# Quarter sums by token, a gate's product spread over the next block's steps, and a rebuilt start in a fused attention and FFN-gate kernel

## The chip, the cores and the metric

The kernel runs on one core of a Trainium2 chip. Its engines, as the profile names them: PE is TensorE (matmuls; PEld is its weight load), DVE is VectorE, ACT is ScalarE, POOL is GpSimd and SP is SyncE, which here only issues DMAs. Each engine runs its own instructions strictly in the order of the program and waits on semaphores for the others. The metric is device time in microseconds (us). Before the change it is 1982.35 us, the median of three runs (1981.34, 1982.35 and 1983.27).

## What is computed

x has 8 sequences of 256 tokens of width 512, 2048 tokens in all. It is normalized per token, goes through an attention with 128 heads and through a feed-forward gate, and the two are multiplied and added to x:

```
xn = (x - mean) / sqrt(var + 1e-5)
s  = attention(xn) @ Wo                    # q, k, v through latents of 64, and a rotary part of 64
lin(x, w, A, B) = x @ tile(w, (1, 4)).T + 0.5 * (x @ A.T @ B.T)       # A, B of rank 2
g  = silu(lin(silu(lin(xn, w1q, a1, b1)) * lin(xn, w3q, a3, b3), w2q, a2, b2))   # 512 -> 1376 -> 512
out = x + s * g
```

The weight matrix w1q has only 128 columns and is repeated four times, so `x @ tile(w1q).T` is (the sum of the four quarters of a token's row) times w1q. These quarter sums appear below. The low-rank part is two numbers per token and matrix, times b1 or b3.

## The kernel before

`first_phase` (L314 to L719) computes everything of the gate and the latents, in four blocks of 512 tokens, and takes about 219 us; the attention behind it, which the change leaves as it is, takes the rest of the 1982. There is no scheduler: the order in which the program emits instructions is the order on each engine. Tiles come from pools in which a name with one or two buffers is reused, so a new tile waits for the last user of the old one. PSUM has eight banks, handed out in turn by `bank`.

The start. `rows` (L357) receives the biases and the first row of each of the two weight matrices by three DMAs on ACT's queue. `warm(26)` (L617) runs 26 idle transposes on PE. Then four matmuls with only two rows, of two passes each (`spread_first`, L626), build "first" tiles that will be subtracted from the weights (`less_first`, `rest_less_first`), for this reason: the normed numbers of a token add up to zero, so a weight's first row can be subtracted from all its other rows. That frees row 0 of the weights and of xs0 and xs1 for the first of the two low-rank numbers (L505); the second is added by DVE (L541, L545). ACT copies the four results from PSUM. DVE gathers mean and variance of the four x tiles (L416, L417) and finds 1/sqrt by a bit shift and three Newton steps (L428 to L438), and norms the four tiles (L459).

Per block `tb` these functions follow each other:

- `load_x` loads four tiles of 128 tokens; `norm` and `norm_one` norm them in place. For blocks 1 to 3 the Newton steps are fourteen small operations on POOL (L440 to L450) and the norming is on ACT (L457).
- `turn` makes 16 PE transposes (L467) and copies them to `act1`, features by tokens.
- `sums` adds the four quarters: two additions on DVE (L479, L481), one on POOL (L480), one copy on ACT (L482), into xs0 and xs1.
- `narrow` (matmuls pm, L497 to L505) finds the low-rank numbers, sends them through DRAM and back as two tiles `low` broadcast to all partitions, and writes them into the first rows of xs0 and xs1.
- `down` (matmuls pp, L511) makes the latents, and `sum_x` has four subtractions on POOL (L158) and their DMAs.
- The loop over `u` = 0 to 5 calls `main(tb, u)`: two chunks (one in step 5) of 128 hidden units. PE makes px and py (L173, eight passes each), DVE adds the second low-rank number, times its column of b, to px (L541, "gate") and py (L545), ACT makes the silu of gate (L544), and POOL (L558) or DVE (L556, L551, L552) multiplies. px and py hold a PSUM bank until DVE has read it.
- `fold` adds four products into one on POOL (L570 to L572), `low_out` makes pm2 (L582).
- `gate_out` (L598) multiplies by w2 (matmuls pf, twelve passes a tile, four tiles), makes a silu on ACT into `gs`, which has two buffers (L608), and stores it (L609). It runs whole at the end of a block.

Among the steps of block `tb` stand the preparations for the next block: the norming of its tiles (steps 2 and 3 in block 0, steps 0 to 3 later), its turn (step 4), and, behind step 5, its `sums`, `narrow` and `down`. Block 3 has instead the first parts of the attention (`Project`, matmuls q) among its steps. `between(n)` puts loads and set-up of the attention at fixed places; `between(0)`, the largest on POOL, follows block 0.

## Time and profile before

| what | value |
|---|---|
| median of three runs | 1982.35 us |
| the profiled execution, its own time | 1983.69 us |
| its span, first to last instruction | 1981.9 us |
| mean granted TensorE clock in it | 0.998 |
| PE busy | 1964.4 us, 99% of the span |
| DVE, ACT, POOL busy | 1575.9, 1098.0, 758.3 us |
| the first matmul of the attention's scores starts at | 218.53 us |
| turn of block 0 starts (first xpt matmul) | 11.03 us |
| loop of block 0 starts (first px matmul) | 23.52 us |
| step 5 of blocks 0 and 1, px starts | 48.31 and 91.78 us |

A line of a group reads: source line, engine, operation, output and inputs by the program's names, count; then busy time, the mean of one in ns, and the idle time before it with what ended it. "PE py <- ACT gs" in the list of waits means that a matmul into py waited for the ACT instruction that works on gs. Matmul ends are modelled and neighbours overlap, so the time between starts is the better measure: eight passes of px or py take 0.86 us from start to start, a transpose 0.109 us at full clock and 0.213 at the start. PEclk is the share of full clock that was granted.

### The profile page before, as it was taken

Reading aid. Unit: us, or ns where it says so; the run is one execution under the profiler, and the core shown is the slowest. Engines: PE = TensorE matmul, PEld = TensorE weight load, DVE = VectorE, ACT = ScalarE, POOL = GpSimd, SP = SyncE. Lnnn points to the kernel's source line nnn. Section 1 sums busy time; section 2 is a strip of 40 time slices with the busy share of each in tenths; the row PEclk is TensorE's granted clock in tenths of the full one; section 3 lists DMA queues with packets and bytes.
Section 4 is the critical chain, followed back from the end, with each engine's and each line's share of the span. In section 5 each row is a group of like instructions: output and inputs, shape, how many; then the busy total and the mean of one; then the engine's idle time right before and its main releaser. Section 6 shows DMA issues by size and latency. Waiting matters only on the chain.

```text
span 1981.9 us, 78697 instructions
## 1 busy us (share of the span) xinstructions
PE 1964.4 (99%) x34033; PEld 1309.7 (66%) x34033; DVE 1575.9 (80%) x2666; ACT 1098.0 (55%) x3029; POOL 758.3 (38%) x1113
## 2 busy tenths in 40 slices
PE   8999999999999999999999999999999999999998
PEld 4334567767777766667776766667776767676775
DVE  7764678888787877788787878788787878888888
ACT  3333465566556555566556555566556555655654
POOL 5877445544552323332332323322332323233232
PEclk9999999999999999999999999999999999999999
DMA  6235322222232223322232322321232222122212
GB/s 195 100 118 179 114 87 87 77 77 87 75 125 89 100 87 101 100 85 68 87 103 89 99 87 101 100 84 69 87 104 88 99 87 86 67 87 87 72 50 87
DMA packets 120017, 187.02 MB, mean 94 GB/s; under 512 B 10715, under 2 KB 84843, under 8 KB 119673
## 3 DMA queue, kind: packets, MB, share of 16 engines
q1 hardware_dynamic: 119665, 181.97, 27.3%
q8 instruction: 270, 4.42, 0.9%
q14 instruction: 74, 0.61, 0.1%
q10 hardware_dynamic: 8, 0.02, 0.0%
HBM read 147.86 MB, written 34.10 MB: 92 GB/s over the span
## 4 chain that ended last, share of the span: by engine, by line
PE 93%; POOL 2%; DVE 2%; issue 1%; DMA 1%; ACT 0%; SPq 0%; POOLq 0%; ACTq 0%; DVEq 0%
PE q L173 40%; PE sc L828 35%; PE av L879 11%; PE po L173 2%; PE pf L173 1%; PE py L173 1%; PE qq L249 1%; PE px L173 1%; POOL h4b L571 0%; POOL hT L558 0%; DVE ring L854 0%; POOL h L570 0%; PE pm L173 0%; DMA xt<-in_x_dram 0%; PE pp L173 0%
## 5 line engine op out<-in xcount | busy, mean ns | idle before, releaser
L847 ACT ACTIVATE pr<-sc,nmx 128x256 f32<-128x256 f32 x2048 | 814.6, 500 | 463.3 <-DVE nmx L841 459.1
L841 DVE TENSOR_REDUCE nmx<-sc 128x2 f32<-128x512 f32 x1024 | 635.5, 683 | 281.7 <-PE sc L828 257.4
L854 DVE STREAM_TRANSPOSE ring<-pr 128x512 f32<-128x512 f32 x1024 | 635.0, 678 | 0.0
L216 POOL TENSOR_TENSOR e<-e,e 128x256 f32<-128x256 f32 x128 | 93.8, 733 | 1042.5 <-ACT e L211 558.8
L173 PE MATMUL q<-x,ws 128*32 128x256 f32 x8192 | 489.0, 379 | 0.7 <-POOL ws L137 0.7
L828 PE MATMUL sc<-act,qr 32*128 32x256 f32 x8192 | 488.3, 374 | 0.0
L828 PEld LDWEIGHTS sc<-act,qr 32*128 32x128 f32 x8192 | 420.7, 185 | 21.8
L173 PEld LDWEIGHTS q<-x,ws 128*32 128x32 f32 x8192 | 266.6, 110 | 176.3 <-POOL ws L137 1.1
L173 PE MATMUL q<-x,w 128*32 128x256 f32 x6144 | 381.7, 381 | 0.9 <-DVE py L545 0.8
L173 PEld LDWEIGHTS q<-x,w 128*32 128x32 f32 x6144 | 187.4, 110 | 155.6 <-ACT pr L847 35.6
L828 PE MATMUL sc<-kc,qcm 32*128 32x256 f32 x4096 | 280.7, 387 | 0.0
L828 PEld LDWEIGHTS sc<-kc,qcm 32*128 32x128 f32 x4096 | 198.0, 184 | 65.0 <-issue 50.4
L879 PE MATMUL av<-ring,vpad 128*32 128x256 f32 (+1 forms) x4160 | 233.4, 376 | 0.1
L211 ACT COPY e<-q 128x256 f32<-128x256 f32 x512 | 202.4, 396 | 26.5 <-PE q L173 26.5
L900 ACT ACTIVATE acc<-av,sides_sb 128x128 f32<-128x128 f32 (+1 forms) x172 | 60.5, 420 | 244.6 <-PE av L879 244.6
L879 PEld LDWEIGHTS av<-ring,vpad 128*32 128x32 f32 x4160 | 134.6, 110 | 88.3 <-issue 1.6
L269 POOL TENSOR_TENSOR qcm<-qc,mask_sb 128x1024 f32<-128x1024 f32 x64 | 122.2, 1910 | 0.0
L217 POOL TENSOR_TENSOR e<-e,e 128x256 f32<-128x256 f32 x128 | 93.6, 731 | 10.0
L218 POOL TENSOR_TENSOR qr<-e,e 128x256 f32<-128x256 f32 x128 | 93.5, 731 | 10.0
L310 POOL COPY vpad<-vall 32x128 f32<-32x128 f32 x256 | 75.4, 294 | 10.2 <-PE av L879 2.3
L228 DVE TENSOR_TENSOR qr<-e,q 128x256 f32<-128x256 f32 x128 | 53.9, 421 | 23.0 <-POOL e L216 17.5
L541 DVE SCALAR_TENSOR_TENSOR gate<-low,bcol_sb,px 128x512 f32<-128x512 f32 x44 | 32.8, 745 | 45.0 <-POOL hT L558 25.7
(124 smaller groups left out, 1138.0 us busy)
## 6 DMA issues: line engine op xcount, KB each, us to landing
w<-in_w_rope_dram SPq DMA_DIRECT2D x128, 512.0 KB
ws<-sums_d SPq DMA_DIRECT2D x96, 512.0 KB
sums_d<-ws SPq DMA_DIRECT2D x32, 512.0 KB
x<-xs_d SPq DMA_DIRECT2D x28, 256.0 KB
xt<-in_x_dram SPq DMA_DIRECT2D x16, 256.0 KB
xs_d<-xt SPq DMA_DIRECT2D x16, 256.0 KB
gate_d<-gs SPq DMA_DIRECT2D x16, 256.0 KB
g<-gate_d SPq DMA_DIRECT2D x16, 256.0 KB
```

Source lines behind the costliest of these rows:

```text
L173: nc.tensor.matmul(to[tile_], w[:, tile_], x, start=start, stop=stop, skip_group_check=True)
L211: nc.scalar.copy(self.e[i], self.banks[i])
L216: nc.gpsimd.tensor_add(m6, m6, m1)
L217: nc.gpsimd.tensor_add(m7, m7, m6)
L218: nc.gpsimd.tensor_add(self.out(1, 1), self.split(m7), self.split(m5))
L269: nc.gpsimd.tensor_mul(qcm, qks[b, sg // 2][0].rearrange("p (q i) -> p q i", i=32).unsqueeze(2).to_broadcast([P, 8, 4, 32]), mask_sb[:, ds ...
L310: nc.gpsimd.tensor_copy(vpad[rows, :, :, 8 * t + 4 * (sg % 2) :][..., :4], valls[b][rows, :, sg])
L828: nc.tensor.matmul(sc[r][:, h, :], lhs.rearrange("p t i -> p (t i)"), rhs, start=(part == 0 and h == 0), stop=(part == 2), skip_group_chec ...
L841: nc.vector.tensor_reduce(nmx[:, r, :], scs[n, f][r], AX.X, ALU.max, negate=True)
L847: nc.scalar.activation(p[:, h, :], scs[n, f][r][:, h, :], AF.Exp, bias=nmxs[n, f][:, r, h : h + 1])
L854: nc.vector.transpose(rings[r][:, (2 * n + f // 2) % 3].rearrange("p k q i -> p q k i")[:, ds(2 * (f % 2), 2)], prs.pop((n, f, r)).rearran ...
L879: nc.tensor.matmul(av[32 * r : 32 * r + 32, cols], vpad[:, k, r, :], rings[r][:, of, k].rearrange("p h q i -> p h (q i)"), start=(k == 0), ...
```

## The change

Four things are edited, all in `first_phase`.

1. The first rows. The biases and first rows of w1 lie in a tile `rows_0`, loaded on ACT's queue, those of w3 in a part of `w2_sb`, loaded on POOL's queue; w2 and b2 are therefore loaded later. 26 idle transposes become 2, and 2 behind the four first-row matmuls become 10. The matmuls go matrix by matrix. The first norm uses ACT's square root, DVE's reciprocal and one Newton step; it stands behind the first three of ACT's copies, and the fourth copy behind it.
2. Block 1's statistics, norming and loads are spread over earlier places. For blocks 2 and 3 `norm` moves from the end of the block before last to step 0.
3. The quarter sums of blocks 1 to 3: `add_quarters` reduces each normed tile from 128x512 to 128x128 on DVE, one step after its norming; behind the turn, in step 4, PE transposes the four results into one bank (`xst`) and ACT copies it twice. The three additions and the copy fall away; block 0 keeps them.
4. `gate_out` of blocks 0 to 2 is done one tile at a time at the head of steps 0 to 3 of the next block; that of block 3 stays whole at the end.

```diff
--- before.py
+++ after.py
@@
         f2 = pool("f2", 2, st)
         xts, xns, xnT, xsum, lows = {}, {}, {}, {}, {}
-        def load_x(tb):
-            xts[tb] = []
-            for n in range(4):
+        def load_x(tb, tiles=range(4)):
+            for n in tiles:
                 t = f1.tile([P, D], F32, tag="xt", name=f"xt_{tb}_{n}", bufs=6)
                 nc.sync.dma_start(out=t, in_=x[ds(tb * TB + n * P, P), :])
-                xts[tb].append(t)
+                xts.setdefault(tb, []).append(t)
@@
 
-        rows = f1.tile([P, 3 * TB], F32, tag="h4", name="rows")[:, 0:F]
-        nc.scalar.dma_start(out=rows[64:97:32], in_=b13[0:33:32, :])
-        for k, wt in enumerate((w1t, w3t)):
-            nc.scalar.dma_start(out=rows[65 + 32 * k : 66 + 32 * k], in_=wt[0:1, :])
+        rows = [
+            f1.tile([P, 3 * TB], F32, tag="h4", name="rows_0")[64:66, 0:F],
+            w2_sb.rearrange("p a m -> p (a m)")[96:98, 0:F],
+        ]
+        for k, (engine, wt) in enumerate(((nc.scalar, w1t), (nc.gpsimd, w3t))):
+            engine.dma_start(out=rows[k][0:1], in_=b13[32 * k : 32 * k + 1, :])
+            engine.dma_start(out=rows[k][1:2], in_=wt[0:1, :])
+
+        one = f2.tile([P, 1], F32, tag="sq", name="one")
+        nc.gpsimd.memset(one, 1.0)
+        nc.scalar.activation(one, one, AF.Sqrt)
         chunk_rows = f2.tile([P, TB], F32, tag="gs", name="chunk_rows")[:, 0:P]
         nc.gpsimd.memset(chunk_rows[0:32], 0.0)
@@
         nc.sync.dma_start(out=wdn_sb, in_=w_down.rearrange("(c p) m -> p c m", p=P))
         for w_sb, wt in ((w1_sb, w1t), (w3_sb, w3t)):
             load_chunks(nc.sync, w_sb, wt)
+        load_x(1, range(2))
...
@@
...
-        load_x(1)
+        load_x(1, range(2, 4))
         mvs = {}
@@
         def norm(tb):
 
-            for n in range(4):
-                norm_part(tb, n)
+            if tb != 1:
+                for n in range(4):
+                    norm_part(tb, n)
             mv = mvs[tb]
             ve = f2.tile([P, 4], F32, tag="ve", name=f"ve_{tb}")
             nc.vector.tensor_scalar_add(ve, mv[:, :, 1], EPS)
-            i0 = f2.tile([P, 4], I32, tag="i0", name=f"i0_{tb}")
-            nc.vector.tensor_single_scalar(i0, ve.bitcast(I32), 1, ALU.logical_shift_right)
-            r0 = f2.tile([P, 4], I32, tag="r0", name=f"r0_{tb}")
-            nc.vector.tensor_scalar(r0, i0, -1.0, float(0x5F3759DF), ALU.mult, ALU.add)
-            r = r0.bitcast(F32)
             e = f2.tile([P, 4], F32, tag="e", name=f"e_{tb}")
-            for step in range(3):
+            if tb:
+                i0 = f2.tile([P, 4], I32, tag="i0", name=f"i0_{tb}")
+                nc.vector.tensor_single_scalar(i0, ve.bitcast(I32), 1, ALU.logical_shift_right)
+                r0 = f2.tile([P, 4], I32, tag="r0", name=f"r0_{tb}")
+                nc.vector.tensor_scalar(r0, i0, -1.0, float(0x5F3759DF), ALU.mult, ALU.add)
+                r = r0.bitcast(F32)
+            else:
+                sq = f2.tile([P, 4], F32, tag="i0", name="sq")
+                nc.scalar.activation(sq, ve, AF.Sqrt)
+                r = f2.tile([P, 4], F32, tag="r0", name="r_first")
+                nc.vector.reciprocal(r, sq)
+            for step in range(3 if tb else 1):
                 new = f2.tile([P, 4], F32, tag=f"r{step}", name=f"r_{tb}_{step}")
                 if tb == 0:
                     nc.vector.scalar_tensor_tensor(e, r, -0.5, r, ALU.mult, ALU.mult)
@@
                 nc.scalar.activation(xn, xn, AF.Identity, bias=off[:, n : n + 1], scale=one)
...
+
+        quarters = {}
+
+        def add_quarters(tb, n):
+            if n == 0:
+                quarters[tb] = f1.tile([P, 4, P], F32, tag="quarters", name=f"quarters_{tb}")
+            nc.vector.tensor_reduce(
+                quarters[tb][:, n], xns[tb][n].rearrange("p (c s) -> p s c", c=4), AX.X, ALU.add
+            )
         def turn(tb):
             a = f1.tile([P, KT, TB], F32, tag="act1", name=f"act1_{tb}")
@@
             a = xnT[tb]
             xs = [f1.tile([P, TB], F32, tag=f"xs{k}", name=f"xs{k}_{tb}") for k in range(2)]
+            xsum[tb] = xs
+            if tb:
+                pt = bank(f"xst_{tb}")
+                for n in range(4):
+                    nc.tensor.transpose(pt[:, ds(n * P, P)], quarters[tb][:, n], ident)
+                for k in range(2):
+                    nc.scalar.copy(xs[k], pt)
+                return
             xs2 = f1.tile([P, TB], F32, tag="tmp", name=f"xs2_{tb}")
             nc.vector.tensor_add(xs[0], a[:, 0, :], a[:, 1, :])
+            norm_part(1, 0)
             nc.gpsimd.tensor_add(xs2, a[:, 2, :], a[:, 3, :])
             nc.vector.tensor_add(xs[0], xs[0], xs2)
             nc.scalar.copy(xs[1], xs[0])
-            xsum[tb] = xs
         def over_xn(tb, name, weights):
             ps = bank(f"{name}_{tb}")
@@
                 t = f1.tile([P, TB], F32, tag=f"low{k}", name=f"low{k}_{tb}")
                 nc.sync.dma_start(out=t, in_=low_d[tb][k : k + 1, :].to_broadcast([P, TB]))
                 lows[tb].append(t)
+            for k in range(2):
                 nc.scalar.copy(xsum[tb][k][0:1], mid[32 * k : 32 * k + 1])
             for j in range(4):
                 nc.sync.dma_start(
@@
                         to, m2[32 * q : 32 * q + 32], 0.5, to, ALU.mult, ALU.add
                     )
-        def gate_out(tb):
-            pfs = [bank(f"pf_{tb}_{n}") for n in range(4)]
+        def gate_out(tb, tiles):
+            pfs = {n: bank(f"pf_{tb}_{n}") for n in tiles}
             for ks in ((0, 1), (2,)):
-                for n in range(4):
+                for n in tiles:
                     for k in ks:
                         on_columns(
                             pfs[n], h4s[tb][:, k, ds(n * P, P)], w2_sb[:, k, :], k == 0, k == 2
                         )
-            for n in range(4):
+            for n in tiles:
                 gs = f2.tile([P, D], F32, tag="gs", name=f"gs_{tb}_{n}")
                 nc.scalar.activation(gs, pfs[n], AF.Silu)
                 nc.sync.dma_start(out=gates_d[4 * tb + n], in_=gs)
@@
             for n in range(count):
                 nc.tensor.transpose(idle[:, ds(n % 4 * P, P)], ident, ident)
-        warm(26)
+        warm(2)
...
-            parts.append(list(by_chunks(to, rows[64 + 32 * k : 66 + 32 * k])))
+            parts.append(list(by_chunks(to, rows[k])))
         def spread_first(k, ps, one, two):
             nc.tensor.matmul(
@@
             )
             return one, ps
-        for i in range(2):
-            for k in range(2):
+        copies = []
+        for k in range(2):
+            for i in range(2):
                 ps = bank(f"first_{k}_{i}").rearrange("p (q m) -> p q m", q=2)
-                nc.scalar.copy(*spread_first(k, ps, *parts[k][i]))
-        warm(2)
+                copies.append(spread_first(k, ps, *parts[k][i]))
+        warm(10)
+        for copy in copies[:3]:
+            nc.scalar.copy(*copy)
+        stats = norm(0)
+        nc.scalar.copy(*copies[3])
         def less_first(k, engine):
             w_sb = (w1_sb, w3_sb)[k]
@@
                 one = w_sb[:, 8:11][:, a, b]
                 nc.gpsimd.tensor_sub(one, one, firsts[k][:, 8:11][:, a, b])
-        stats = norm(0)
         for n in range(4):
             norm_one(0, n, *stats)
         turn(0)
         sums(0)
+        norm_part(1, 1)
         less_first(0, nc.gpsimd)
         narrow(0)
         less_first(1, nc.vector)
+        norm_part(1, 2)
+        norm_part(1, 3)
         between(-1)
-        for to, of in ((a2_sb, a2), (w2_sb, w2t), (w2_sb[96:98, 2, :], b2[0:2, :])):
-            nc.sync.dma_start(out=to, in_=of)
+        nc.sync.dma_start(out=a2_sb, in_=a2)
         down(0)
         ps = bank("bcol")[:, 0:32]
         nc.tensor.transpose(ps, chunk_rows[0:32], ident[0:32, 0:32])
         nc.scalar.copy(bcol_sb.rearrange("p c k -> p (c k)"), ps)
         rest_less_first(0)
         rest_less_first(1)
+        for to, of in ((w2_sb, w2t), (w2_sb[96:98, 2, :], b2[0:2, :])):
+            nc.sync.dma_start(out=to, in_=of)
+        stats = norm(1)
         for tb in range(NTB):
             more = tb + 1 < NTB
             for u in range(6):
+                if tb and u < 4:
+                    gate_out(tb - 1, [u])
                 pj = None
                 if not more and u >= 2:
                     pj = Project(u - 2)
@@
                 if u in (3, 5):
                     fold(tb, u // 2 - 1)
                     low_out(tb, u // 2 - 1)
-                if u == 1 and tb == 0:
-                    stats = norm(1)
                 if more:
                     for n in range(4):
-                        if u == (n if tb else 2 + n // 2):
+                        if u == (min(n + 1, 3) if tb else n) + 1:
+                            add_quarters(tb + 1, n)
+                    if u == 0 and tb:
+                        stats = norm(tb + 1)
+                    for n in range(4):
+                        if u == (min(n + 1, 3) if tb else n):
                             norm_one(tb + 1, n, *stats)
                 if u == 4 and more:
                     turn(tb + 1)
+                    sums(tb + 1)
                 if u == 1 and tb + 2 < NTB:
                     load_x(tb + 2)
                 if tb == NTB - 2 and u == 1:
@@
                 if not more:
                     between(u + 2)
             if more:
-                sums(tb + 1)
                 narrow(tb + 1)
                 low_out(tb, 2)
                 down(tb + 1)
             else:
                 low_out(tb, 2)
-            gate_out(tb)
+                gate_out(tb, range(4))
             if tb == 0:
                 between(0)
-            if tb + 2 < NTB:
-                stats = norm(tb + 2)
         nc.scalar.activation(cks_sb, cks_sb, AF.Exp)
         between(8)
```

## The prediction

> **What bounds the kernel now.** I read the page's busy table and chain first, then the busy time by stretch, then TensorE's (PE's) waits, then the order in time at the places that these name.

> The page, busy time and chain:

> ```profile
> span 1981.9 us, 78697 instructions
> PE 1964.4 (99%) x34033; PEld 1309.7 (66%) x34033; DVE 1575.9 (80%) x2666; ACT 1098.0 (55%) x3029; POOL 758.3 (38%) x1113
> PE 93%; POOL 2%; DVE 2%; issue 1%; DMA 1%; ACT 0%; SPq 0%; POOLq 0%; ACTq 0%; DVEq 0%
> ```

> PE is the bound, so a gain can only come out of its holes, and a new hole costs in full. By stretch (PE busy, then the other engines, PEclk, DMA share, GB/s):

> ```profile
> 0.00:11.00 11.00, 9.16 (x36) 5.89 (x36) 5.86 (x22) 3.53 (x5) 4.29 (x31) 0.89 0.88 236
> 11.00:24.00 13.00, 12.97 (x133) 7.79 (x137) 8.57 (x12) 4.63 (x12) 8.17 (x7) 0.83 0.46 143
> 24.00:59.00 35.00, 31.01 (x313) 10.80 (x309) 26.90 (x45) 13.29 (x23) 25.66 (x39) 1.00 0.46 149
> 59.00:102.00 43.00, 41.43 (x408) 14.62 (x404) 30.10 (x48) 17.00 (x28) 36.05 (x70) 1.00 0.34 114
> 102.00:146.00 44.00, 42.34 (x424) 14.99 (x420) 29.89 (x48) 17.00 (x28) 30.27 (x37) 1.00 0.40 133
> 146.00:219.00 73.00, 70.35 (x1008) 29.73 (x1004) 31.00 (x46) 23.93 (x50) 52.95 (x61) 1.00 0.42 144
> 219.00:1982.00 1763.00, 1757.17 (x31742) 1225.87 (x31736) 1443.59 (x2447) 1018.57 (x2886) 600.94 (x873) 1.00 0.27 89
> ```

> The rows are the start, the head of block 0, blocks 0 to 3, and the attention, which the edits leave alone. Up to 219 us PE idles 13.7 us, of which the head has 1.9 and block 0 has 4.0. PE's waits there (us, times, longest):

> ```profile
> PE py L173 <- ACT gs L608: 2.3, 2, 1.4
> PE py L173 <- DVE gate L541: 1.7, 1, 1.7
> PE px L173 <- DVE gate L541: 1.6, 3, 0.6
> PE q L173 <- DVE py L545: 0.8, 1, 0.8
> PE pf L173 <- DVE h L594: 0.5, 2, 0.3
> PE xpt L467 <- DVE xt L459: 0.4, 1, 0.4
> ```

> Waits on gs are the two-buffer store of the gate; waits on L541 and L545 are chunks whose PSUM banks DVE has not freed. The head in order of time (start, duration):

> ```profile
> 1.35 4.86 PE L615 MATMUL idle<-ident 128*128 128x128 f32 x26 [1.35 <-POOL ident masks.py:199]
> 6.13 3.87 PE L627 MATMUL first<-rows,others 2*128 2x512 f32 x8
> 11.03 3.68 PE L467 MATMUL xpt<-ident,xt 128*128 128x128 f32 x16 [0.41 <-DVE xt L459]
> ```

> and the group of first-row passes from 8.5 to 14.5 us (busy, mean ns):

> ```profile
> L627 PE MATMUL first<-rows,others 2*128 2x512 f32 x2 | 1.7, 954 | 0.0
> ```

> Idle transposes start 0.213 us apart up to 5.0 us, 0.109 after; the late first-row passes take 954 ns where earlier ones stood 0.43 apart. PEclk is 0.50 from 8.6 to 15.2, although PE was busy for 3.19 of the 3.30 us before 8.4, mostly with these two-row passes.

> **The change, part by part.** Durations are of this execution. It took 1983.69, 1.34 above the median 1982.35; I add the sum to the median.

> *Head.* The rows of the first tile land at 4.74 (biases at 3.87), instead of 7.23 for the last row. 26 idle transposes become 2, so the eight passes can start at about 4.8, but on a PE at half rate: 0.43 doubled is 0.86, and 0.954 was seen, so 6.9 to 7.6 us, to 11.7 to 12.4. The ten transposes behind them are 10 x 0.213 = 2.1, and the turn of block 0 starts at 13.8 to 14.5 instead of 11.03. The square root stands on ACT behind three copies, the third of which waits for six passes: 4.8 + 5.2 + 0.6 = 10.6. With root, reciprocal and one step (five small operations of 0.2) the rows are normed from 11.6 against 10.43, before PE asks for them: the nine Newton operations removed (8.66 to 10.39, 1.7 us) buy nothing. After 15.3 the clock was full in this trace; I take the same, since ten transposes and the turn fill the time ahead of it. Seven of 16 transposes then run at 0.213 and the rest at 0.109, so pm starts at about 16.4 instead of 14.64, while 0.33 that pm lost at half rate comes back. With the later passes +1.5 to +2.3: **+1.9**. Bounds: -1.0 if the passes run at 0.43 (they end at 8.3, rows normed from 9.3, turn at about 10, still at 0.213), +5 if the clock comes one step of 3.4 us later (the full times 5.1, 8.5, 15.3 are 3.4 apart or twice that). The POOL queue's two row loads have no row in this trace; ACT's issues took 0.21 to 1.10 and landed 2.9 to 3.1 later. These passes come third and fourth, after 8.2, so a load from POOL has 5 us beyond ACT's first landing to hide in; nothing, up to +1 if it takes twice ACT's time.

> [...]

> *Block 0.* Statistics of block 1 (four of 0.83) leave step 1 for places before the loop; DVE begins the loop 1.2 later (25.95 for 24.73). Newton for block 1 runs on POOL after the last subtraction: that queue is without a gap to 30.23, then 14 x 0.28 = 3.9, to 34.1. ACT's norm of tile 0 (0.75) waits for it, ahead of step 1's silu (0.63): step 1's product starts at 35.55. From there DVE has 12 gates and ups (0.66 apart), 7 products (0.68) and 4 quarter sums before the turned sums: 7.9 + 4.8 + 4 x 0.68 = 15.4, to 50.95. The quarter sum has no row here; the nearest is DVE's reduction of 128x512 (L841, 683 ns), which I take; bounds 0.35 and 1.35 (POOL's and DVE's large subtractions took 1.3). In the new order px of step 5 stands behind four transposes of these sums: 51.3 instead of 48.32. 0.5 of later holes (0.31 at 48.8, and part of its wait) closes: **+2.5**; down to 0 if the sums take 0.35 and POOL is earlier, +5 at 1.35.

> *Blocks 1 and 2.* Gone: waits for gs (0.74 and 1.1), pf's wait for the fold (0.4 and 0.46), because gate_out runs a tile at a time (1.29 us) at the head of steps 0 to 3. Its sixteen DMAs and silus are spread over the same queues; SP waits 23 us for gs now with nothing due behind. New: in step 4, PE has 1.74 of turn and 0.44 of sums' transposes, then waits. DVE after the last py: 0.66 + four products 2.7 + two sums 1.36, and 0.44 and latencies: 5.3. It comes to that late by 0.5 at least: step 3's product and sum (1.4) stand before step 4's first gate, whose matmul comes 0.86 later. So px of step 5 starts 5.8 after the last py, against 3.0 and 2.4 before. Hole, less what is gone and less the px and py holes of before (0.76, 0.66, 0.3): **+1.4 and +1.6**. Bounds -1.5 each (sums ready when the turn ends) and +3 each (DVE 3 us behind, as at 89.66, where it begins a gate whose matmul ended at about 86.4). POOL's and ACT's removed sums were beside other work: nothing.

> *Block 3.* No turn, no sums, and gate_out(2) is spread: 1.57 (gs), 1.05 (q behind py) and 0.44 (pf) go; gate_out(3) at the end stays with its 0.37: **-3.1**; bounds -3.1 and -1.

> Sum: +1.9 + 2.5 + 1.4 + 1.6 - 3.1 = +4.3, so 1982.35 + 4.3 = 1986.6.

> **Rivals.** (a) *The clock falls in the new holes.* Each leaves PE without work for some 3.6 us; the longest now is 1.87. A stretch of 3.4 us at half rate costs 1.7; in two of three blocks 3.4: 1990.0. For it: it fell at 8.5 with PE busy on small work. Against: 1.87 never did it. [...]

> (b) *First rows at full rate.* PEclk reads 1.00 from 0 to 8.5, so the 0.213 of the first transposes may be another thing than the clock. Head -1.0 instead of +1.9: 1983.7.

> (c) *Faster: the sums are not late.* 1.29 us more of PE work in each of steps 0 to 3 lets DVE run ahead (its gates waited 25.7 us for POOL's products), and sums land as the turn ends. Blocks 1 and 2 give -1.5 each, block 0 -0.5, with the head at +1.9 and block 3 at -3.1: -4.7, 1977.7. Each us by which the sums are earlier is worth 3 us; it decides when px of step 5 starts less than 2.5 after the last py. Against: the DVE work behind the last py adds up to 4.7 with no lateness at all.

> **How the numbers follow.** Forecast 0.47 (1984.5 to 1988.7), (a) 0.20, (b) 0.18, (c) 0.15. A measurement of this kernel tells about 0.2%, 3.96 us, from no change: same is 1978.4 to 1986.3. The forecast gives 0.28 slower and 0.19 same, (a) slower, (b) same, (c) 0.13 faster: faster 0.13, same 0.39, slower 0.48. Range from (c), a little cut, to (a): 1978.5 to 1990.5.

> **What would show it.** Right: eight first-row passes 0.86 to 0.95 apart from 4.8; the turn at 13.8 or later; PE waiting for DVE's quarter sum at the new transposes in blocks 0 to 2, some 3 to 3.6 us each; no wait for gs in blocks 1 to 3. Wrong: passes at 0.43, turn before 11; that wait below 1 us; PEclk below 1.00 after 24 us; a late row load from POOL that holds the third pair of passes.

## The result, and the profile after

The changed kernel takes 1996.55 us, median of six runs (1994.41 to 1998.07), against 1982.14 for the kernel before (six runs, 1981.34 to 1983.27). The ratio is 1.0073, with a 95% interval of 1.0063 to 1.0083: it is slower by 14.4 us, where 4.3 were forecast, and the time lies above the range. The side was right and the size was not.

The profiled execution of the changed kernel took 1995.62, 0.9 under its median. Its busy times on the page, and the busy time by stretch (PE, PEld, DVE, ACT, POOL, then PEclk, DMA share, GB/s):

```profile
span 1993.8 us, 78696 instructions
PE 1971.9 (99%) x34029; PEld 1318.6 (66%) x34029; DVE 1581.7 (79%) x2665; ACT 1100.6 (55%) x3034; POOL 754.5 (38%) x1113
```

```profile
0.00:11.00 11.00, 7.88 (x16) 3.77 (x17) 5.34 (x16) 3.93 (x7) 5.61 (x34) 1.00 0.92 252
11.00:24.00 13.00, 13.00 (x143) 8.44 (x145) 10.41 (x18) 5.35 (x14) 8.68 (x8) 1.00 0.51 136
24.00:59.00 35.00, 28.07 (x240) 9.33 (x236) 28.42 (x42) 13.40 (x22) 22.02 (x36) 0.85 0.45 146
59.00:102.00 43.00, 39.85 (x368) 12.91 (x364) 30.09 (x47) 16.36 (x27) 34.17 (x68) 0.95 0.35 114
102.00:146.00 44.00, 41.32 (x403) 14.07 (x395) 30.30 (x49) 17.06 (x29) 26.57 (x34) 0.97 0.40 133
146.00:219.00 73.00, 72.23 (x1026) 37.71 (x1029) 31.15 (x47) 23.59 (x48) 44.27 (x51) 0.96 0.39 130
```

PE is as busy as before, 99%, and that hides the loss: a PE at half clock is busy too. What tells is the column behind the engines, PEclk. It was 1.00 in the last four rows before and is 0.85, 0.95, 0.97 and 0.96 now. (The rows are cut where the blocks of the kernel before end. Up to the attention the granted clock was 0.50 three times, from 46.7 to 56.9, from 97.9 to 104.7 and from 145.7 to 152.5 us; the third time belongs to block 2.) And the largest of the waits behind the start, with one at the start (us, times, longest):

```profile
PE xst L505 <- DVE quarters L480: 9.8, 5, 3.5
PE first L659 <- POOL others L375: 1.8, 1, 1.8
PE xpt L490 <- DVE gate L573: 1.0, 1, 1.0
```

The waits for gs, for q behind py and for the fold are gone, as forecast; in their place stands one new wait, for the quarter sums, three times. Block 1 in order of time (start, duration), PE first and then DVE in the same stretch:

```profile
92.32 1.03 PE L173 MATMUL py<-xs,w_sb 128*32 128x512 f32 x8
93.28 1.97 PE L490 MATMUL xpt<-ident,xt 128*128 128x128 f32 x16
95.08 0.38 PE L505 MATMUL xst<-ident,quarters 128*128 128x128 f32 x2
98.14 0.47 PE L505 MATMUL xst<-ident,quarters 128*128 128x128 f32 x1 [2.68 <-DVE quarters L480]
99.09 0.47 PE L505 MATMUL xst<-ident,quarters 128*128 128x128 f32 x1 [0.47 <-DVE quarters L480]
99.49 1.94 PE L173 MATMUL px<-xs,w_sb 128*32 128x512 f32 x8
101.20 1.93 PE L173 MATMUL py<-xs,w_sb 128*32 128x512 f32 x8
102.91 1.94 PE L614 MATMUL pm<-hT,a_sb 128*32 128x512 f32 x8
```

```profile
96.36 0.69 DVE L584 TENSOR_TENSOR hT<-gate,py 32x512 f32<-32x512 f32 x1
97.07 1.96 DVE L480 TENSOR_REDUCE quarters<-xt 128x128 f32<-128x512 f32 x2
```

DVE comes to the last two quarter sums at 97.07, behind step 4's four products, and PE, whose turn ended at about 95.1, waits until 98.14 and 99.09. Then px and py of step 5 take 1.71 us from start to start instead of 0.86. That is half clock, and it holds until 104.7:

```profile
99.50:104.70 5.20, 5.20 (x29) 1.26 (x32) 1.83 (x3) 1.70 (x3) 0.00 (x0) 0.50 0.00 0
104.70:110.00 5.30, 5.30 (x88) 2.55 (x84) 1.80 (x3) 0.77 (x2) 3.99 (x4) 1.00 0.01 3
```

Block 2 repeats this, with the same waits of 2.68 and 0.47. In block 0 the wait is 3.53, from 48.2 to 51.74, but there the clock was already down when it began, at 46.7, behind two shorter waits of the turn:

```profile
44.47 0.63 PE L490 MATMUL xpt<-ident,xt 128*128 128x128 f32 x4 [0.78 <-DVE hT L588]
46.08 0.63 PE L490 MATMUL xpt<-ident,xt 128*128 128x128 f32 x4 [0.98 <-DVE gate L573]
51.74 0.48 PE L505 MATMUL xst<-ident,quarters 128*128 128x128 f32 x1 [3.53 <-DVE quarters L480]
```

The balance by stretch, from the starts of PE's instructions in the two profiled executions (a block runs from the end of its own pp, for block 0 from its first px, to the end of the next block's pp; block 3 to the first scores):

| stretch | before | after | difference | forecast |
|---|---|---|---|---|
| start, to the first px | 23.5 | 22.8 | -0.7 | +1.9 |
| block 0 | 35.5 | 42.1 | +6.6 | +2.5 |
| block 1 | 43.5 | 47.6 | +4.1 | +1.4 |
| block 2 | 43.0 | 47.7 | +4.6 | +1.6 |
| block 3 | 73.0 | 71.0 | -2.0 | -3.1 |
| attention | 1763.4 | 1762.7 | -0.7 | 0 |

The sum is 11.9. The profiled execution of before was 1.6 above its median and that of the changed kernel 0.9 below; that makes up the 14.4.

### The profile page after: what moved, and what is told of

The parts are those of the page before. It is cut to its first block, busy times and chain, and to the rows that moved or that the text cites. A ratio compares the mean times of both kernels' runs of the same rounds, so it can differ in the third digit from the quotient of the medians.

```text
span 1993.8 us, 78696 instructions
## 1 busy us (share of the span) xinstructions
PE 1971.9 (99%) x34029; PEld 1318.6 (66%) x34029; DVE 1581.7 (79%) x2665; ACT 1100.6 (55%) x3034; POOL 754.5 (38%) x1113
## 4 chain that ended last, share of the span: by engine, by line
PE 95%; DVE 2%; POOL 1%; issue 1%; DMA 0%; ACT 0%; POOLq 0%; DVEq 0%; ACTq 0%
PE q L173 39%; PE sc L872 34%; PE av L923 11%; PE po L173 2%; PE pf L173 2%; PE px L173 1%; PE py L173 1%; PE qq L249 1%; PE pm L173 1%; PE pp L173 1%; PE pm L614 0%; DVE ring L898 0%; PE vps L294 0%; DVE py L577 0%; PE first L659 0%
## 5 line engine op out<-in xcount | busy, mean ns | idle before, releaser
L173 PE MATMUL q<-x,ws 128*32 128x256 f32 x8192 | 491.0, 379 | 0.4 <-issue 0.3
L173 PEld LDWEIGHTS q<-x,ws 128*32 128x32 f32 x8192 | 269.2, 110 | 174.7 <-issue 0.8
L173 PE MATMUL q<-x,w 128*32 128x256 f32 x6144 | 383.0, 381 | 0.0
L173 PEld LDWEIGHTS q<-x,w 128*32 128x32 f32 x6144 | 190.2, 110 | 152.5 <-ACT pr L891 35.8
```

What stands on the lines that cost most here:

```text
L173: nc.tensor.matmul(to[tile_], w[:, tile_], x, start=start, stop=stop, skip_group_check=True)
```

## The experiments

The theory after the result, A: PE runs out of work at the xst transposes in three blocks, and the clock falls to half in each of these holes. Its rivals: B, the loss sits in the start or is spread over the engines, and the holes only show it; and the prediction's own view, that holes cost their length and nothing more. All times are medians beside runs of the kernel before on the same chip.

### The hole filled with idle work

```diff
                 pt = bank(f"xst_{tb}")
+                for n in range(30):
+                    nc.tensor.transpose(pt[:, ds(n % 4 * P, P)], ident, ident)
                 for n in range(4):
```

> The changed kernel, with 30 idle transposes (3.3 us at full clock) ahead of the four xst transposes in each of three blocks: the wait stays as long, but PE is busy in it. Theory A: the clock does not fall, so about 2.6 us come back in each block, 7.8 in all: 1988.7, between 1987 and 1991, and px and py of step 5 take 0.86 instead of 1.71. If the half rate comes from something else than the idle time (the work that follows, or the transposes themselves, which in the start of the kernel did lift the clock), nothing comes back: 1996.5, or more by what the 30 transposes add.

1988.91, ratio to before 1.0033 (1.0020 to 1.0045). Against the changed kernel 7.6 us come back, although PE reaches step 5 no earlier (7.1 us after the start of the last py in blocks 1 and 2 beside 7.2, and 11.0 beside 10.6 in block 0). The stretches around the same place in block 1:

```profile
93.00:98.00 5.00, 4.71 (x42) 4.36 (x40) 4.61 (x6) 1.95 (x5) 4.75 (x5) 1.00 0.63 210
98.00:103.00 5.00, 5.00 (x71) 2.25 (x74) 2.88 (x4) 1.70 (x3) 0.34 (x1) 1.00 0.02 3
```

PEclk is 1.00 through the filled hole and behind it in blocks 1 and 2. In block 0 the clock falls at the turn here too, at 47.3, but it is back at 50.7, within the idle transposes, where in the changed kernel it stayed down until 56.9 (PEclk over 24.00:59.00 is 0.95 here and 0.85 there). So 7.6 of the 14.4 are the clock, some 2.5 a block, and here idle time is what brings it down or keeps it down: with PE at useless work in the same wait, PEclk was 1.00 in blocks 1 and 2.

With ten idle transposes in place of the thirty, a third of the hole:

> The changed kernel, with 10 instead of 30 idle transposes ahead of the xst transposes: 1.1 us of the hole are filled and some 2 us in blocks 1 and 2 (2.9 in block 0) stay empty. If the clock falls only after idle time about as long as 3 us, it holds in two or three blocks: 1989 to 1991.5. If it takes far less than that (any such hole in a window that counts busy time), it falls as in the changed kernel: 1996.5, with px and py of step 5 again at 1.71.

1990.33, ratio 1.0044 (1.0030 to 1.0057). In its profile, that of the fastest of its five runs (1988.3 to 1994.2), holes of 1.8 and 0.8 us are left in blocks 1 and 2, and the clock holds there (PEclk 1.00). In the kernel with two additions below it fell behind holes of 1.8 and 0.6, and in block 0 of the changed kernel behind waits of 0.78 and 0.98. So the length of a hole alone does not decide.

A longer stretch tells more than a single hole. Counted from the first change of the granted clock, at 5.08 us in the trace of the kernel before and at 12.55 in that of the changed kernel, the ten later changes of these two traces lie on a grid of 3.41 us. Three windows of this grid in the changed kernel (those ahead of its three falls), two with ten idle transposes (the hole of block 1), and one in a kernel below (with two additions); PE's busy time stands behind the comma:

```profile
43.27:46.68 3.41, 1.65 (x12) 1.02 (x10) 3.31 (x6) 1.60 (x3) 3.33 (x4) 1.00 0.52 154
94.47:97.88 3.41, 0.99 (x10) 0.76 (x7) 3.32 (x5) 1.85 (x4) 3.27 (x4) 1.00 0.84 264
142.26:145.67 3.41, 0.77 (x8) 0.53 (x5) 3.32 (x6) 1.61 (x4) 3.19 (x5) 1.00 0.00 0
```

```profile
92.22:95.63 3.41, 2.31 (x22) 2.07 (x19) 3.32 (x6) 2.08 (x5) 3.27 (x4) 1.00 0.73 254
95.64:99.05 3.41, 2.33 (x18) 0.82 (x22) 1.96 (x3) 0.59 (x1) 1.57 (x2) 1.00 0.14 53
```

```profile
95.15:98.56 3.41, 1.43 (x12) 0.48 (x4) 3.30 (x6) 0.00 (x0) 2.15 (x3) 1.00 0.13 49
```

PE idled 1.8, 2.4 and 2.6 us in the first three windows, and the clock fell at the end of each. It idled only 1.1 and 1.1 in the next two, which meet in the middle of the hole at 95.6, and the clock held. It idled 2.0 in the last, which took in a whole hole of 1.8 and 0.6, and the clock fell. In the traces of the kernel before and of the changed one, behind the start, five windows at full clock ended with a fall, with 1.76, 2.42 and 2.64 us of idle time and, at the two kernels' ends, 2.21 and 3.28; the other 1144 idled 1.33 or less, and the clock held. That is what these two executions show, and no limit for others.

### The sums behind step 5

```diff
                     turn(tb + 1)
-                    sums(tb + 1)
...
             if more:
+                sums(tb + 1)
                 narrow(tb + 1)
```

> The changed kernel, with the turned quarter sums (the four xst transposes and ACT's two copies) moved from step 4 to behind step 5, where the additions stood before; the quarter sums on DVE stay where they are. Theory A (the holes at the xst transposes, and the half clock that each leaves behind, make the loss): both go. The trace of the changed kernel gives 9.8 us of waits for the quarter sums and some 2.6 us lost at half rate after each of three holes, 7.8; together 17.6, so 1996.55 - 17.6 = about 1979, between 1976 and 1982, with PEclk 1.00 after 24 us. Theory B (the loss sits in the start or is spread over the engines, and the holes only show it): less than 5 us come back, 1992 or more.

1981.37, ratio 0.9996 (0.9987 to 1.0006): 15.2 us come back, more than the whole loss, and the kernel stands level with before. This settles A against B: nothing else of the change was touched. A had one thing wrong: in block 0 the clock falls ahead of the hole, and the hole only keeps it down. Taken as a difference, the 7.6 of the clock leave 7.6 for the waiting itself. It came out 2.4 above the 1979 that I expected: block 0 still has waits at its turn (0.78 and 0.99), and the clock is at half in step 5 there: px starts 1.71 ahead of py (48.03 and 49.74), and PEclk over 24.00:59.00 is 0.95.

### Each part alone

The start alone:

```diff
-        warm(26)
+        warm(2)
...
-        warm(2)
+        warm(10)
+        for copy in copies[:3]:
+            nc.scalar.copy(*copy)
+        stats = norm(0)
+        nc.scalar.copy(*copies[3])
```

(with the two row tiles on two queues, the square root and the later loads of w2, as in the change's diff)

> The kernel before, with the start of the changed kernel alone: first rows in two tiles on two queues, 2 and 10 idle transposes, square root, w2 loaded later. Theory A: the start gains what the trace of the changed kernel shows, the loop of block 0 beginning at 22.77 instead of 23.52: 1981.4, within 0.5. The prediction had +1.9 for this part, 1984.0. A start that costs more than that in most runs, because the clock comes one step later, would give 1985 or more.

1983.70, ratio 1.0008 (0.9999 to 1.0017): not told from no change. My expectation, taken from one trace of the changed kernel, missed. The changed start against the old one once more, where both have the sums behind step 5:

> The changed kernel, with the start of the kernel before and with the sums behind step 5. The start alone cost 1.3 beside before, so 1981.37 - 1.3 = 1980.1, between 1979 and 1982. If the new start is no loss in company with the others: 1981.4 or more.

1981.27 with the old start (ratio to before 0.9995, 0.9986 to 1.0005), 1981.37 with the new one: no difference. Over the profiles of this study the first px starts at 22.8 to 24.1 us with the old start and at 22.8 to 24.6 with the new one; in the trace of the changed kernel the full clock comes at 12.55 us and the first px at 22.77. Whether the later px belong to later clocks was not shown.

The spread gate alone:

```diff
             for u in range(6):
+                if tb and u < 4:
+                    gate_out(tb - 1, [u])
                 pj = None
...
-            gate_out(tb)
+                gate_out(tb, range(4))
```

> The kernel before, with gate_out of blocks 0 to 2 a tile at a time at the head of steps 0 to 3 of the next block, and nothing else. Theory A: the waits for gs (0.74, 1.1, 1.57), for q behind py (1.05) and for the fold (0.39, 0.46, 0.44) go, at most 5.75 us; block 3 of the changed kernel gave 2.0 of its 3.1, so I expect -4.5: 1977.6, between 1976.4 and 1980. If the spread silus and stores hold ACT and PSUM banks at the wrong time: 1982 or more, with new waits for px or py in steps 0 to 3.

1994.16, ratio 1.0060 (1.0045 to 1.0075): slower by 11.8 where I expected a gain of 4.5. Its waits:

```profile
PE pf L173 <- DVE h L594: 7.5, 2, 3.7
PE pf L173 <- issue: 5.4, 1, 5.4
```

and the place in block 1, PE and then DVE:

```profile
106.22 1.90 PE L173 MATMUL pf<-w_sb,h 128*32 128x512 f32 x16
111.86 1.06 PE L173 MATMUL pf<-w_sb,h 128*32 128x512 f32 x8 [3.74 <-DVE h L594]
112.71 1.75 PE L173 MATMUL px<-xs,w_sb 128*32 128x512 f32 x8
```

```profile
105.04 1.75 DVE L481 TENSOR_TENSOR xs<-xs,xs 128x512 f32<-128x512 f32 x1 [3.76 <-POOL xs L480]
106.83 0.75 DVE L497 TENSOR_SCALAR mid<-pm,cks_sb 128x512 f32<-128x512 f32 x1
109.57 2.14 DVE L594 SCALAR_TENSOR_TENSOR h<-pm,h 32x512 f32<-32x512 f32 x3 [1.99 <-ACT h L592]
```

The third part of a tile's product needs the low-rank sums that DVE finishes with L594. DVE is held up before that by the additions of the quarters, which wait for POOL's addition behind three folds. Done whole, gate_out has the first two parts of all four tiles to do meanwhile; done one tile at a time, it stands still for 5.5, 3.9 and 3.9 us, and the half clock comes behind these holes too (px 1.75; PEclk 0.62 from 112 to 116 us). In the changed kernel the additions are gone, and so is this wait. The other way round, the quarter sums without the spread gate:

> The kernel before, with the quarter sums by token, in step 4 as in the changed kernel, and the earlier norming that they need; the start and the whole gate_out are those of before. If the parts of the change added up, this one would be worth 14.4 - 1.3 (the start alone) - 11.8 (the spread gate alone) = +1.3: 1983.7. Theory A (the sums in step 4 make the loss, whatever the others do; the spread gate alone lost by another wait, pf for DVE's last low-rank sum, which the additions on POOL and DVE hold up and which goes with them): the whole 15.2 that moving the sums gave back, so 1997.5, between 1995 and 1999, with three waits of xst for the quarter sums and half clock behind them, and no wait of pf for L594 above 1 us.

2002.53, ratio 1.0104 (1.0086 to 1.0122), 20.3 slower than before, and above the range that I gave:

```profile
PE xst L492 <- DVE quarters L467: 12.8, 5, 4.0
PE xpt L477 <- DVE gate L560: 3.0, 3, 1.0
PE xpt L477 <- DVE hT L575: 2.3, 3, 0.8
```

The waits for the quarter sums and at the turn are longer here, in all three blocks. My reading, which no run tests, is that DVE is later still without the 2.57 us of pf in each of steps 0 to 3. The parts alone are worth +1.3, +11.8 and +20.3, and together +14.4: the spread gate and the quarter sums each cost less beside the other, and neither can be priced from the kernel before by itself.

### A cheaper quarter sum

The reduction of a tile took longer than I had assumed; the range and median of its durations (ns):

```profile
L480 DVE TENSOR_REDUCE quarters<-xt x12: 1021/1062/1105, 36.2 to 145.6; 128x128 f32<-128x512 f32 x12
```

To see what the term is worth, two additions in its place:

```diff
-            nc.vector.tensor_reduce(
-                quarters[tb][:, n], xns[tb][n].rearrange("p (c s) -> p s c", c=4), AX.X, ALU.add
-            )
+            nc.vector.tensor_add(half, xns[tb][n][:, 0 : 2 * P], xns[tb][n][:, 2 * P : 4 * P])
+            nc.vector.tensor_add(quarters[tb][:, n], half[:, 0:P], half[:, P : 2 * P])
```

> The changed kernel, with each reduction of a tile (1.06 us on DVE) done as two additions instead, of 256 and of 128 columns; by DVE's additions of 512 columns (0.69) they should take some 0.36 and 0.22, 0.6 with the gap. It tests the term that the prediction had too small. DVE has 0.45 less a tile: the hole in blocks 1 and 2 shrinks by two of them (0.9, from 2.9 and 0.8 to about 2.8 in all), block 0 by up to four (1.8). If only the waits shrink and the clock falls as before: 1996.55 - 3.6 = 1993. If the clock holds in blocks 1 and 2, where filled_10 left holes of 1.75 and 0.83 and it held: another 5, 1988.

1997.72, ratio 1.0080 (1.0065 to 1.0095): no gain against the changed kernel's 1.0073. The additions are cheap only at times. DVE at one place and at a later one, then POOL at the first:

```profile
88.69 0.48 DVE L483 TENSOR_TENSOR half<-xt 128x256 f32<-128x256 f32 x1
89.21 1.26 DVE L484 TENSOR_TENSOR quarters<-half 128x128 f32<-128x128 f32 x1
...
103.37 0.41 DVE L483 TENSOR_TENSOR half<-xt 128x256 f32<-128x256 f32 x1
103.82 0.29 DVE L484 TENSOR_TENSOR quarters<-half 128x128 f32<-128x128 f32 x1
```

```profile
87.61 2.72 POOL L592 TENSOR_TENSOR hT<-gate,hT 128x512 f32<-128x512 f32 x2 [1.58 <-ACT gate L578]
```

The second addition takes 0.29 at the later place and 1.26 at the first, where POOL is in a product; there it ends at 90.47, 0.14 after POOL's at 90.33. Another long one, from 95.05 to 96.33, ends 0.15 after POOL's L605, which was running when it started and ended at 96.18; the twelve take 0.29 to 1.29, with a median of 1.26. The reductions have no such spread (1.02 to 1.11, beside POOL or not). So a duration read from a quiet place was again too small, and the test could not price the term.

### A version that beats both

The sums behind step 5 left some waits. Filling the turn of block 1 with repeated transposes, with the old start:

```diff
-                for c in range(KT):
+                for c in list(range(KT)) * (3 if tb == 1 and n else 1):
```

> As old_start_sums_behind, and in the turn of block 1 the transposes of tiles 1 to 3 are done three times over (the same data into the same bank, 0.87 us more a tile), where PE otherwise waits 0.94, 1.15 and 0.76 for banks. The profile of the kernel with the sums behind step 5 shows the clock at half for px and py of step 5 in block 0, 1.3 us lost. If the clock holds through the filled waits: 1978.8. If not, or if the longer turn holds up ACT's copies: 1980.1 to 1981.

1980.80, ratio 0.9992 (0.9982 to 1.0002): PEclk in block 0 is 1.00 in its profile, but the 0.5 us gained over 1981.27 are not told from nothing. With the two additions for the reductions it lost:

> old_start_repeat (old start, sums behind step 5, transposes of block 1's turn repeated), with the two additions for each reduction. The waits of xst behind step 5 (0.84 in blocks 1 and 2, 1.0 in block 0) and part of DVE's lag in block 0 go: 1980.8 - 2.5 = 1978.3, between 1977 and 1980. If the additions are no cheaper than the reduction: 1980.8.

1987.13, ratio 1.0030 (1.0019 to 1.0042); nine of its twelve second additions take 1.24 to 1.29, PE waits 5.1 us for the sums instead of 2.1, and the clock falls once behind them, at 98.6. And with the first tile normed a step later in block 0:

> As two_additions, and in block 0 the norming of tile 0 moves from step 0 to step 1, its quarter sum to step 2, so that ACT's silus of step 1 no longer stand behind the Newton steps on POOL (DVE waited 1.8 for them, PE 0.7 to 1.0). 0.7 to 1.0 less than two_additions: 1977.4. If DVE's stream is then simply as late by step 4: no change.

1985.34, ratio 1.0021 (1.0012 to 1.0030): 1.8 better than without, though the two intervals overlap, so that the edit looks good and is not proven. The last kernel goes back to the reduction, keeps this edit, and puts the turned sums behind the pm matmuls:

```diff
             nc.vector.tensor_scalar_mul(mid, over_xn(tb, "pm", ck_sb), cks_sb[:, 0:1])
+            if tb:
+                sums(tb)
...
-                        if u == (min(n + 1, 3) if tb else n):
+                        if u == (min(n + 1, 3) if tb else max(n, 1)):
```

> old_start_repeat (old start, reductions on DVE as in the changed kernel), with the turned sums one place later still, behind the pm matmuls of narrow, and with tile 0 of block 1 normed in step 1 and summed in step 2. The traces of the sums behind step 5 show 0.84 of waiting for the quarter sums in blocks 1 and 2 and 1.0 in block 0: pm's 3.45 would cover all three, 2.7. The later norming was worth 1.8 beside the two additions: 1980.8 - 2.7 - 0.8 = 1977.3, between 1976 and 1979. If narrow's row copies, which now stand behind the sums' copies on ACT, hold up the next block: 1980 or more, with px of step 0 waiting for xs.

1976.72 (ten runs, 1975.88 to 1978.37) beside 1981.27 for before; ratio 0.9977, 0.9967 to 0.9986. It is faster than the kernel before by 4.6 us and, by the two ratios, than the changed one by some 19, with the same quarter sums and the same spread gate. Against the kernel with the repeated transposes the two ratios make it some 3 us; how much of that is the new place and how much the later norming was not separated. Up to 219 us PE waits for next to nothing, and the clock holds:

```profile
PE idle L636 <- POOL ident masks.py:199: 1.4, 1, 1.4
PE pf L173 <- issue: 0.7, 1, 0.7
PE first L648 <- DMA rows<-in_w3t_dram: 0.5, 1, 0.5
PE pf L173 <- POOL h L593: 0.2, 1, 0.2
```

```profile
24.00:59.00 35.00, 35.00 (x355) 14.87 (x351) 31.91 (x48) 16.65 (x28) 27.45 (x41) 1.00 0.50 167
59.00:102.00 43.00, 43.00 (x428) 18.36 (x424) 31.14 (x49) 17.46 (x29) 35.75 (x70) 1.00 0.35 123
102.00:146.00 44.00, 44.00 (x437) 20.49 (x433) 32.48 (x51) 18.48 (x31) 28.42 (x35) 1.00 0.44 147
```

## Why the prediction was wrong

*The clock.* The step that failed is the forecast's choice to price the holes by their length and to leave the clock to rival (a) at 0.20: the sum had nothing for it, and it took 7.6 us. The waits of blocks 1 and 2 were forecast well: px of step 5 was to start 5.8 after the last py ended and started 6.3 after in block 1 (99.49 against 93.18), with holes of 3.7 together (2.8 and 0.8, from the starts) against 3.6. But the clock fell in all three blocks, not in two, and a fall cost 2.5 and not 1.7: it stayed down for 6.8 us in blocks 1 and 2 and for 10.2 in block 0, and about 5 us of work behind each hole ran at half rate (99.5 to 104.7), not 3.4. Rival (a)'s sum with three blocks at the measured price, 1986.6 + 7.6 = 1994.2, is within 2.4 of the result. A fall did not need a hole as long as the 3.6 that I had forecast: no single wait ahead of the fall in block 0 was longer than 0.98, and in the kernel with two additions it fell behind 1.8 and 0.6. I had weighed "1.87 never did it", which is true of the kernel before and says nothing of 3.6; there no window of the grid between the start and the attention had more than 1.33 us of idle time.

*Block 0, +2.5.* 6.6 in the trace. The half clock has 2.5 of it, less the 0.5 of later waits that closed as forecast. px of step 5 came 4.6 late, counted from the first px, and not 3.0: each quarter sum took 1.06, where L841's 0.683 was taken from a reduction that reads PSUM and writes two numbers a partition, and four of them make 1.5. The rest of the chain (POOL's Newton steps before ACT's first norm) went as said: the trace has ACT waiting 4.28 us for them, until 33.59.

*Blocks 1 and 2, +1.4 and +1.6.* 4.1 and 4.6, of which the clock has about 2.5 each; without it the terms hold to 0.5. One figure on the way was wrong: a tile of pf is 2.57 us, not 1.29. It had no weight in the sum, since all tiles were counted as moved, but it made rival (c) look worse than it was. Another was PE's idle time up to 219 us: its rows add up to 11.7 and not 13.7; nothing rests on it.

*POOL's and ACT's removed sums, "nothing".* True for the whole gate_out and false for the spread one: the part alone shows that the spread gate needs them gone (11.8 us). The forecast for the two together was right in that the gs and fold waits vanished.

*Start, +1.9.* The start is worth nothing that could be told (1983.70 alone, 0.1 in company); the first of these tests, with an interval of -0.2 to +3.4, does not exclude 1.9, but the way there was another. It was built on first-row passes from 4.8 and a turn at 13.8 or later. They started at 3.80, when POOL's last memset of `others` for them ended (3.75); the rows were there, from two short issues on ACT's queue (0.51 and 0.22 us, where the one issue for the two biases had taken 1.10). Three of the eight stood 0.49, 0.36 and 0.63 from the next instead of 0.86, and the turn began at 12.03. Rival (b) fell: the other passes stood 0.85 apart (the first 1.0), half rate, though PEclk reads 1.00 over the start (the record of the clock begins with its first change, at 12.6). The rows on POOL's queue landed 3.7 and 3.8 us after their issues and held up nothing that shows.

*Block 3, -3.1.* -2.0 in this trace, -2.8 and -1.0 in the profiles of the kernel with the sums behind step 5 and of its old-start twin. The named waits are gone in all; short waits of the scores' preparation, different in each execution, take some of it back. I leave those open.

*Rival (c)*, the sums not late, was the right idea at the wrong place: they are late in step 4, and two places further down they are not, for 1976.72 where (c) had 1977.7. That the two numbers are so close is luck: (c) has the new start, and no repeated transposes and no later norming.

## What to carry to other kernels

On an engine that is busy 99% of the time, a new wait can cost more than its length: here, behind 2.68 and 0.47 us of waiting, the next 5.2 ran at half rate (PEclk 0.50). Look at the granted clock, since the busy share does not show it, and add up idle time that lies close together instead of going hole by hole: in the changed kernel the clock fell behind waits of 0.78 and 0.98 in one window of 3.41 us, and in the kernel before it held behind one of 1.68. A cross-engine result should be consumed after work that is already there to cover it: the same sums cost 15 us where PE asked for them at once, nothing behind step 5, and were part of a gain of 4.6 behind the pm matmuls. And parts of a change that shift load between the same engines can't be priced one by one: here +11.8 and +20.3 belong to parts that gain together.
